# An attention and sign feed-forward kernel: three kinds of transposes leave TensorE, and the feed-forward is computed from three bf16 parts

## The chip, the cores and the metric

The kernel runs on one core of a Trainium2 chip. The time is that of one execution on the device, in microseconds (us). The names of the engines are those of the profile: PE is TensorE (PEld its weight loads), DVE is VectorE, ACT is ScalarE, POOL is GpSimd, SP is SyncE, which here only issues DMAs. Before the change the median of 3 runs is 4421.93 us (4421.24 to 4422.01).

## The reference

The input `x` has 4 batches of 2048 rows of 512 values, all in float32. There are 16 heads of 32 columns.

```python
q = (x @ Wq.T).reshape(N, S, H, hd).transpose(0, 2, 1, 3)      # k and v alike
attn = softmax(q @ k.T / sqrt(hd), axis=3)
x = layernorm(x + (attn @ v).transpose(0, 2, 1, 3).reshape(N, S, D))
w = (weights >= 0.0) * 2.0 - 1.0                               # 512 x 512, only +1 and -1
y = clip(einsum('bsi,oi->bso', x, w) * scale + bias, -100, 100)
out = layernorm(x + y)
```

`scale` and `bias` have one value for each of the 512 output columns.

## The kernel before

**Tiles and steps.** The work is cut into 16 groups `n` (4 batches of 4 groups of 4 heads), each group into 4 blocks `qb` of 512 queries, each block into 16 chunks `kc` of 128 keys. One chunk of one block is a *step*; there are 1024 steps, 64 to a group. The loop at the end of the function (L742 to L777) writes the instructions of one step after the other, and every engine works through its own in that order.

**What a step holds.** `scores` (L302) puts four banks of scores, transposed, into PSUM: a bf16 matmul that adds minus the row maximum, `negm`, and an f32 matmul of keys and queries. ACT turns them into `p` with four exponentials. `max_unit` (L236) computes scores once more, for a step 22 steps ahead (`LEAD`), the other way round, so that DVE can reduce each row to its maximum: three of the four banks are reduced out of PSUM, the fourth is first copied to SBUF (`moved`) by ACT. In every second step `weighted` (L323) multiplies two `p` by the values, and DVE adds the result to `oT`. POOL adds the `p` of a block up (`add_up`, L345), 14 additions of 128x2048 values for each 16 steps; of the sum and the last `p`, a matmul with ones makes the denominators.

PSUM has eight banks. `take` hands out the bank that a small model expects to be free first.

**Three things that are transposed on PE.** `max_rows` (L285) turns the maxima of a block, split by `max_parts` into three bf16 parts that are summed by the matmul, into `negm`: four bf16 transposes and an ACT copy. It stands three steps ahead of the block. `reciprocals` (L394) turns the denominators `dT` with four f32 transposes, so that DVE can take their reciprocals by query; `add_attention` (L410) turns `oT` likewise, multiplies, adds the columns of `x` and stores the result in DRAM (`res`). `Finish.turn` (L495) turns 128 rows for the feed-forward with four f32 transposes.

**The end of a batch.** `finish` (L550) spreads the rest of a batch, both layer norms and the feed-forward, over the steps of the next batch: 4 row tiles of 128 for each block, one tile each 13 steps (11 for the third batch). For a tile, `norm` (ACT), `turn` (PE, ACT), then three times `ffn` (L505), each a third of the output columns: four f32 matmuls, each of which the profile shows as two, and three DVE operations, of which each reads or writes the bank in PSUM. The signs of the weights are multiplied by `scale` beforehand by POOL (`sign_weights`, L145). The last batch has its own, denser plans: `finish_last` (L571) and, for its last block, `finish_end` (L600).

**Order.** `task` puts work on a list, with a first and a last step; `plan` (L680) deals it out to the steps: up to two *big* tasks (projections, thirds) and one *small* one in odd steps, a *col* task (denominators) in even ones. A third is kept apart from other thirds by `on_vector`. `at` fixes work to the end of a step. SP has the DMAs in program order; one that waits holds those behind it.

Of the kernel before, what the change touches and what calls it, by code (L numbers as in the profile page):

```python
# [20 lines left out]
def kernel(  # L21
# [13 lines left out]
    P = 128  # L35
# [21 lines left out]
    stage = ctx.enter_context(tc.tile_pool(name="stage", bufs=4))  # L57
# [9 lines left out]
    work = ctx.enter_context(tc.tile_pool(name="work", bufs=2))  # L67
# [37 lines left out]
    ident_bf = const.tile([P, P], BF16, name="ident_bf")  # L105
    nc.vector.tensor_copy(ident_bf, ident)
# [38 lines left out]
    def sign_weights():  # L145

        ws = raws["ws"]
        nc.gpsimd.tensor_scalar(ws, ws, 0.0, 2.0, ALU.is_ge, ALU.mult)
        for oc in range(DC):
            nc.gpsimd.tensor_scalar(  # L150
                ws[:, oc, :], ws[:, oc, :], 1.0, scale_t[:, oc : oc + 1], ALU.subtract, ALU.mult
            )

    raws = {n: load_weight(w, n) for n, w in (("wk", wk), ("wq", wq))}
    scale_t = const.tile([P, DC], F32, name="scale_t")
    bias_bc = const.tile([P, D], F32, name="bias_bc")

    def load_rest():
        for n, w in (("wv", wv), ("ws", w_ffn)):
            raws[n] = load_weight(w, n)  # L160
        nc.sync.dma_start(out=scale_t, in_=ffn_scale.rearrange("(c p) -> p c", p=P))
        nc.sync.dma_start(out=bias_bc, in_=ffn_bias.partition_broadcast(P))
# [15 lines left out]
    rec = {}  # L178

# [95 lines left out]
    def max_parts(n, qb, i):  # L275
        part = parts.pop((n, qb))
        nm = cols_of(i, NTQ, HG)
        sp = split[qb % 2]
        nc.vector.tensor_reduce(nm, part, AX.X, ALU.min)
        nc.vector.tensor_copy(sp[:, :, :, 0], nm)  # L280
        nc.vector.tensor_tensor(nm, nm, sp[:, :, :, 0], ALU.subtract)
        nc.vector.tensor_copy(sp[:, :, :, 1], nm)
        nc.vector.tensor_tensor(sp[:, :, :, 2], nm, sp[:, :, :, 1], ALU.subtract)

    def max_rows(n, qb):  # L285
        sp = split[qb % 2]
        i = take()
        pt = ps[:, i, : QB // 2].bitcast(BF16)
        for qc in range(NTQ):
            nc.tensor.transpose(  # L290
                pt[:, ts(qc, P)], sp[:, qc, :, :].rearrange("p h d -> p (h d)"), ident_bf
            )
        negm[n, qb] = small.tile([P, QB], BF16, tag="negm", name="negm")
        runs("full", 0.23)
        nc.scalar.copy(negm[n, qb], pt)
        give(i, "ACT", 0.6)
# [76 lines left out]
    def denominators(n, qb):  # L373

        if is_last(n, qb):
            b = sums[0]
        else:
            b = take()
            ones_times(b, last_p.pop((n, qb)), True, False)
            ones_times(b, acc.pop((n, qb)), False, True)  # L380
        dT = once.tile([P, QB], F32, tag="dT", name="dT")
        nc.scalar.copy(dT, ps[:, b, :])
        give(b, "ACT", 0.6)
        acc[n, qb] = dT

# [7 lines left out]

    def reciprocals(n, qb):  # L394
        i, pd = turn_back(acc.pop((n, qb)))
        rec[n, qb] = small.tile([P, NTQ, HG, 1], F32, tag="rec", name="rec")
        nc.vector.reciprocal(rec[n, qb], pd[:, :, :, 0:1])
        give(i, "DVE", 0.3)
# [30 lines left out]
    class Finish:  # L429
        def __init__(self, b, g):  # L430
            self.b, self.g = b, g
            self.mv, self.rs, self.nb, self.nT, self.rows_rs = {}, {}, {}, {}, {}

# [60 lines left out]

        def turn(self, j):  # L495
            i = take()
            pt = cols_of(i, DC, P)
            for c in range(DC):
                nc.tensor.transpose(pt[:, c, :], self.row(j)[:, ts(c, P)], ident)  # L499
            runs("full", 0.44)  # L500
            self.nT[j] = work.tile([P, DC, P], F32, tag="nT", name="nT", bufs=4)
            nc.scalar.copy(self.nT[j], pt)  # L502
            give(i, "ACT", 0.6)

        def ffn(self, j, third):  # L505
            cols = slice(0, D) if third is None else slice(THIRDS[third], THIRDS[third + 1])
            i = take()
            py = ps[:, i, : cols.stop - cols.start]
            for c in range(DC):
                nc.tensor.matmul(  # L510
                    py, lhsT=self.nT[j][:, c, :], rhs=wT["ws"][:, c, cols],
                    start=(c == 0), stop=(c == DC - 1),
                )
            runs("full", 6.8e-3 * (cols.stop - cols.start))
            nc.vector.tensor_tensor(py, py, bias_bc[:, cols], ALU.add)
            nc.vector.tensor_scalar(py, py, MAX_VAL, -MAX_VAL, ALU.min, ALU.max)
            dst = self.row(j)[:, cols]
            nc.vector.tensor_tensor(dst, dst, py, ALU.add)
            give(i, "DVE", 0.5 + 3.1e-3 * (cols.stop - cols.start))
# [30 lines left out]
    def finish(b, qb, a, every, w, lag):  # L550
        f = Finish(b, qb)
        at(a, f.load)
        for j in range(NTQ):
            at(a + 2 + j, f.stats, 1, j)
        at(a + 6, f.rstd, 1)
        at(a + 7 + lag, f.shift, 1)
        for j in range(NTQ):
            t = a + 8 + lag + every * j
            at(t, f.norm, 1, j)
            turned = task("small", t + 1, t + 3, f.turn, j)  # L560
            for k in range(3):
                task("big", t + 2, t + w, f.ffn, j, k, after=turned)
            at(t + w, f.stats, 2, j)
        e = a + 9 + lag + every * (NTQ - 1) + w
        at(e, f.rstd, 2)
        at(e + 1 + lag, f.shift, 2)
        for j in range(NTQ):
            at(e + 2 + lag + j, f.norm, 2, j)
        at(e + 5 + lag, f.store)

    def finish_last(qb, last):  # L571

        f = Finish(B - 1, qb)
        at(last - 9, f.load_last)
        a = last + 7
        late = qb == NQB - 2
        for j in range(NTQ):
            at(a + j // 2, f.stats, 1, j)
        at(a + 2, f.rstd, 1)
        at(a + 4, f.shift, 1)  # L580
        ffns = []
        for j in range(NTQ):
            t = a + 5 + (j if late else 2 * j)
            by = t + 6
            at(t, f.norm, 1, j)
            if late:
                by = total + (-1, 1, 4, 5)[j]
            turned = task("small", t + 1, t + 3, f.turn, j, after=ffns[j - 2] if j > 1 else None)
            for k in [None] if late else range(3):
                ffn = task("big", by if late else t + 2, by, f.ffn, j, k, after=turned)  # L590
            ffns.append(ffn)
            at(by + late, f.stats, 2, j)
        e = total + 7 if late else a + 18
        at(e, f.rstd, 2)
        at(e + 2, f.shift, 2)
        for j in range(NTQ):
            at(e + 3 + j, f.norm, 2, j)
        at(e + 7, f.store)

    def finish_end(qb, last):  # L600
# [10 lines left out]
        for j in range(NTQ):  # L611
            t = total + (6, 6, 7, 8)[j]
            turned = task("small", t, t, f.turn, j)
            t = total + 7 + j
            task("big", t, t, f.ffn, j, None, after=turned)
            at(t, f.stats, 2, j)
            at(t, f.rstd, 2, j, j + 1)
            at(t + 1, f.shift, 2, j, j + 1)
            at(t + 1, f.norm, 2, j)
            at(t + 1, f.store_tile, j)  # L620
# [7 lines left out]
    at(-8, sign_weights)  # L628
    for n in range(N):
# [28 lines left out]
        for qb in range(NQB):  # L658
# [3 lines left out]
            task("small", first - 3, first - 3, max_rows, n, qb)  # L662
# [4 lines left out]
            t = task("small", d + 1, d + 1 + w, reciprocals, n, qb, after=t)  # L667
            e = d + 2 if is_last(n, qb) else d + 3
            task("small", d + 2, e + w, add_attention, n, qb, after=t)
            if g == NG - 1:  # L670
                if b < B - 1:
                    every = 13 if b < B - 2 else 11
                    finish(b, qb, (b + 1) * NG * STEPS + qb * (5 * every - 1), every, every, 3)
                else:
                    (finish_end if is_last(n, qb) else finish_last)(qb, last)

    def on_vector(t):
        return t[3].__name__ == "ffn"

    def plan(quota=None):  # L680
# [9 lines left out]
        while any(len(gone[kind]) < len(tasks[kind]) for kind in tasks):  # L690
# [10 lines left out]
            for kind in most:  # L701
# [8 lines left out]
                if kind == "big" and middle:  # L710
                    if quota is not None and not heavy:
                        k = max(1, min(k, -(-quota[group] * (at_n + 1) // STEPS) - used[group]))


                    thirds = [t for t in can if on_vector(t)]
                    can = [t for t in can if not on_vector(t)]
                    if thirds and not can:
                        can = thirds[:1]
                    elif thirds and k == 2 and not heavy and not any(map(on_vector, must)):
                        can = thirds[:1] + can  # L720
                picked = must + can[: max(0, k - len(must))]
                for t in sorted(picked, key=lambda t: not on_vector(t)):
# [9 lines left out]
    for _ in range(4):  # L732
# [8 lines left out]
    s = start  # L741
    while s <= max(*chosen, *behind):  # L742
        now = None
# [70 lines left out]
```

## Time and profile before

| what | value |
|---|---|
| median of 3 runs | 4421.93 us |
| the profiled execution's own time | 4420.69 us |
| its span, first to last instruction | 4418.7 us |
| PE busy | 4380.8 us, 99% |
| POOL busy | 4083.3 us, 92%; 889 additions of 4.54 us are 4034.0 |
| DVE busy | 3320.2 us, 75% |
| ACT busy | 3048.4 us, 69% |
| granted PE clock | 0.999 |
| feed-forward matmuls on PE (L510) | 259.3 us busy |
| transposes on PE: rows (L499), sums and outputs (L390), maxima (L290) | 41.8, 83.6, 25.3 us busy |

Matmuls are pipelined, so that busy times of PE overlap and are longer than what a matmul adds to the chain. A group of instructions is told by its line, its engine and its tiles (`out<-in`). An idle time is put down to what ended it. The chain of work that ended last is followed back from the last instruction and shows what the time consists of.

### The profile page before, as it was taken

How to read it: one execution, taken by the hardware profiler on the slowest of the kernel's cores; microseconds unless marked ns; L12 is line 12 of the kernel's file. 1: busy time of each engine (PE TensorE's matmuls, PEld its weight loads, DVE VectorE, ACT ScalarE, POOL GpSimd, SP SyncE). 2: the span in 40 equal slices, each digit the busy share in tenths (PEclk: the TensorE clock that was granted, in tenths of full speed). 3: DMA queues.
4: the chain of work that ended last, by engine and by line, in shares of the span. 5: the costliest groups of instructions: out<-in, count | busy, mean ns of one | idle time of the engine just before them, and what ended most of it. 6: DMA issues, size and time to landing. Idle time of an engine off the chain costs nothing.

```text
span 4418.7 us, 94451 instructions
## 1 busy us (share of the span) xinstructions
PE 4380.8 (99%) x38648; PEld 2261.4 (51%) x38648; DVE 3320.2 (75%) x5909; ACT 3048.4 (69%) x6493; POOL 4083.3 (92%) x940
## 2 busy tenths in 40 slices
PE   9999999999999999999999999999999999999998
PEld 5554444454555555555555555555555555555443
DVE  6777777777777777777777777777777777777774
ACT  5666666676667667677676766767667676767675
POOL 3999999999999999999999999999999999999994
PEclk9999999999999999999999999999999999999999
DMA  3000000010000000011000000001000000000001
GB/s 91 6 11 11 6 11 11 9 39 28 6 11 30 6 20 20 6 42 32 20 20 6 30 11 16 20 7 48 16 20 20 18 18 20 16 20 30 13 23 45
DMA packets 98019, 92.30 MB, mean 21 GB/s; under 512 B 4272, under 2 KB 73904, under 8 KB 97584
## 3 DMA queue, kind: packets, MB, share of 16 engines
q1 hardware_dynamic: 92304, 82.07, 6.2%
q8 instruction: 302, 4.95, 0.5%
q10 hardware_dynamic: 5280, 4.19, 0.3%
q14 instruction: 133, 1.09, 0.1%
HBM read 53.74 MB, written 32.51 MB: 20 GB/s over the span
## 4 chain that ended last, share of the span: by engine, by line
PE 89%; POOL 8%; ACT 1%; issue 1%; DVE 1%; DMA 0%; ACTq 0%; POOLq 0%; DVEq 0%
PE ps L330 19%; PE ps L247 18%; PE ps L312 18%; PE ps L206 15%; POOL acc L350 8%; PE ps L306 7%; PE ps L510 5%; PE ps L356 3%; PE ps L390 2%; PE ps L499 1%; PE ps L195 1%; ACT p L319 1%; DVE part L254 1%; PE ps L290 0%; ACT xg_last L489 0%
## 5 line engine op out<-in xcount | busy, mean ns | idle before, releaser
L350 POOL TENSOR_TENSOR acc<-acc,p 128x2048 f32<-128x2048 f32 x825 | 3743.2, 4537 | 106.1 <-ACT p L319 49.3
L319 ACT ACTIVATE p<-ps 128x512 f32<-128x512 f32 x4096 | 2115.0, 604 | 1148.4 <-PE ps L312 1113.8
L254 DVE TENSOR_REDUCE part<-ps 128x1 f32<-128x512 f32 x3072 | 1934.8, 684 | 821.1 <-PE ps L247 820.2
L247 PE MATMUL ps<-kT,qT 32*128 32x512 f32 x8192 | 1098.1, 590 | 0.0
L312 PE MATMUL ps<-qT,kT 32*128 32x512 f32 x8192 | 1070.7, 590 | 0.0
L330 PE MATMUL ps<-p,vv 128*32 128x512 f32 x8192 | 983.6, 598 | 0.5 <-ACT p L319 0.3
L247 PEld LDWEIGHTS ps<-kT,qT 32*128 32x128 f32 x8192 | 524.0, 185 | 379.8 <-issue 221.0
L254 DVE TENSOR_REDUCE part<-moved 128x1 f32<-128x512 f32 x1024 | 691.2, 675 | 1.7 <-ACT moved L266 1.6
L266 ACT COPY moved<-ps 128x512 f32<-128x512 f32 x1024 | 634.5, 620 | 21.8 <-PE ps L247 16.7
L330 PEld LDWEIGHTS ps<-p,vv 128*32 128x32 f32 x8192 | 220.3, 109 | 685.6 <-issue 346.5
L306 PE MATMUL ps<-negm,ones_bf 32*128 32x512 bf16 x4096 | 434.9, 384 | 3.9 <-ACT p L319 1.3
L312 PEld LDWEIGHTS ps<-qT,kT 32*128 32x128 f32 x8192 | 405.6, 184 | 38.3 <-issue 20.4
L350 POOL TENSOR_TENSOR acc<-p 128x2048 f32<-128x2048 f32 x64 | 290.8, 4544 | 132.4 <-ACT p L319 132.3
L342 DVE TENSOR_TENSOR oT<-ps,oT 128x512 f32<-128x512 f32 x448 | 309.8, 692 | 90.1 <-PE ps L330 57.6
L306 PEld LDWEIGHTS <-ones_bf 32*128 32x128 bf16 x4096 | 104.3, 91 | 496.9 <-issue 438.3
L206 PEld LDWEIGHTS ps<-wvT,xT 128*128 128x128 f32 x2048 | 244.6, 191 | 67.7 <-ACT p L319 62.1
L206 PE MATMUL ps<-wvT,xT 128*128 128x128 f32 x2048 | 270.3, 280 | 1.4 <-ACT p L319 0.5
L206 PEld LDWEIGHTS ps<-xT,wkT 128*128 128x128 f32 x2048 | 242.4, 191 | 48.2 <-ACT p L319 46.7
L206 PE MATMUL ps<-xT,wkT 128*128 128x128 f32 x2048 | 265.1, 279 | 0.5 <-ACT p L319 0.2
L206 PE MATMUL ps<-xT,wqT 128*128 128x128 f32 x2048 | 262.2, 277 | 1.1 <-ACT p L319 1.0
L510 PE MATMUL ps<-wsT,nT 128*128 128x172 f32 (+2 forms) x1408 | 259.3, 329 | 2.4 <-ACT nT L502 1.1
L206 PEld LDWEIGHTS ps<-xT,wqT 128*128 128x128 f32 x2048 | 245.2, 192 | 25.5 <-ACT p L319 23.0
(74 smaller groups left out, 1831.2 us busy)
## 6 DMA issues: line engine op xcount, KB each, us to landing
xs<-in_L_attn_x_dram SPq DMA_DIRECT2D x64, 256.0 KB, 2.8
xc<-in_L_attn_x_dram SPq DMA_DIRECT2D x60, 256.0 KB, 3.2
res<-xc SPq DMA_DIRECT2D x60, 256.0 KB, 2.4
xg<-res SPq DMA_DIRECT2D x12, 1024.0 KB, 6.1
out_dram<-xg SPq DMA_DIRECT2D x12, 1024.0 KB, 4.8
xg_last<-res SPq DMA_DIRECT2D x4, 768.0 KB, 6.1
out_dram<-xg_last SPq DMA_DIRECT2D x3, 1024.0 KB, 4.3
raw_wk<-in_L_attn_Wk_dram ACTq DMA_DIRECT2D x4, 256.0 KB, 6.3
```

The lines of the kernel that those rows point to most:

```text
L206: nc.tensor.matmul(pp, lhsT=lhs(c), rhs=rhs(c), start=(c == 0), stop=(c == DC - 1))
L247: nc.tensor.matmul(ps[:, banks[h], :], lhsT=qT[n, qb][rows, ts(qc, P)], rhs=kT[n][rows, ts(kb, QB)], start=True, stop=True,)
L254: nc.vector.tensor_reduce(part[:, qc, h : h + 1, kb], src, AX.X, ALU.max, negate=True)
L266: nc.scalar.copy(moved, ps[:, banks[-1], :])
L306: nc.tensor.matmul(ps[:, banks[h], :], lhsT=ones_bf[rows, :], rhs=negm[n, qb][rows, :], start=True, stop=False,)
L312: nc.tensor.matmul(ps[:, banks[h], :], lhsT=kT[n][rows, ts(kc, P)], rhs=qT[n, qb][rows, :], start=False, stop=True,)
L319: nc.scalar.activation(p[:, h, :], ps[:, banks[h], :], AF.Exp, scale=SM_SCALE)
L330: nc.tensor.matmul(pb[cols, :], lhsT=vv[n][:, kc, cols], rhs=p[:, h, :], start=(i == 0), stop=(i == 1),)
L342: nc.vector.tensor_tensor(outs[n, qb], pb, outs[n, qb], ALU.add)
L350: nc.gpsimd.tensor_tensor(a, before if kc == 1 else a, p, ALU.add)
L356: nc.tensor.matmul(ps[h * HD : (h + 1) * HD, b, :], lhsT=ones, rhs=p[:, h, :], start=start, stop=stop,)
L510: nc.tensor.matmul(py, lhsT=self.nT[j][:, c, :], rhs=wT["ws"][:, c, cols], start=(c == 0), stop=(c == DC - 1),)
```

## The change

- **Maxima.** `max_parts` ends with a DMA transpose on SP's queue, 128x512 bf16, that writes `negm`. `max_rows`, its PE transposes and its ACT copy are gone.
- **Sums of the keys.** The denominators are copied over the first quarter of the sum's own tile; a DMA writes one row of each head to DRAM, a second reads them back as single values, turned. `reciprocals` stands two steps after the denominators. The last block of all keeps the PE transposes.
- **Feed-forward.** 56 of 64 row tiles: the normalized row is split into three bf16 parts (two ACT copies, two DVE subtractions), a DMA transposes all three (128x1536), and a third is 12 bf16 matmuls with the signs, which bf16 holds exactly. ACT copies a third to SBUF; three entries in the plan then scale it, add the bias and clip it, and add it to the row, on DVE. The last eight tiles keep the f32 way (`turn`, `ffn_whole`) with signs and scale in one.
- **Signs.** 12 DVE operations from step 80 on, in place of five of POOL's at the start.
- **Plan.** A tile each 12 steps (10 for the third batch), the pieces of a tile in steps of their own; the planner no longer treats thirds apart. `stage` has three buffers instead of four, `work` one instead of two.

```diff
-    stage = ctx.enter_context(tc.tile_pool(name="stage", bufs=4))
+    stage = ctx.enter_context(tc.tile_pool(name="stage", bufs=3))
-    work = ctx.enter_context(tc.tile_pool(name="work", bufs=2))
+    work = ctx.enter_context(tc.tile_pool(name="work", bufs=1))
...
+    def sign_weights(ic, k):
+        w = wT["ws"][:, ic, :]
+        if k == 0:
+            nc.vector.tensor_scalar(w, w, 0.0, 2.0, ALU.is_ge, ALU.mult)
+        elif k == 1:
+            nc.vector.tensor_scalar(ws_bf[:, ic, :], w, 1.0, None, ALU.subtract)
+        else:
+            nc.vector.tensor_tensor(w, ws_bf[:, ic, :], scale_bc, ALU.mult)
...
         nc.vector.tensor_tensor(sp[:, :, :, 2], nm, sp[:, :, :, 1], ALU.subtract)
-    def max_rows(n, qb):
...
+        nc.sync.dma_start_transpose(
+            out=negm[n, qb].rearrange("p (t q) -> p t q", t=NTQ),
+            in_=sp.rearrange("p t h d -> p (t h d)"),
+        )
...
+            dT = whole[:, 0, :]
         nc.scalar.copy(dT, ps[:, b, :])
         give(b, "ACT", 0.6)
         acc[n, qb] = dT
+        if not is_last(n, qb):
+            columns_of_sums(n, qb)
+            at(step[0] + 2, reciprocals, n, qb)
...
+    def columns_of_sums(n, qb):
+        dT = acc.pop((n, qb))
+        rows = dram.tile([HG, QB], F32, tag="sums", name="sums", bufs=2)
+        nc.sync.dma_start(out=rows, in_=dT.rearrange("(h r) q -> h r q", h=HG)[:, 0, :])
+        sums_of[n, qb] = small.tile([P, HG * NTQ], F32, tag="sums", name="sums")
+        with nc.allow_non_contiguous_dma(reason="2048 single sums"):
+            nc.sync.dma_start(
+                out=sums_of[n, qb], in_=rows.rearrange("h (t p) -> p (h t)", p=P)
+            )
...
+            by_head = sums_of.pop((n, qb)).rearrange("p (h t) -> p t h", h=HG)
+            nc.vector.reciprocal(rec[n, qb][:, :, :, 0], by_head)
...
+        def part_high(self, j):
+            self.parts[j] = work.tile([P, 3, D], BF16, tag="parts", name="parts")
+            nc.scalar.copy(self.parts[j][:, 0, :], self.row(j))
...
+        def less_high(self, j):
+            self.left[j] = work.tile([P, D], F32, tag="left", name="left")
+            nc.vector.tensor_tensor(
+                self.left[j], self.row(j), self.parts[j][:, 0, :], ALU.subtract
+            )
...
+        def part_middle(self, j):
+            nc.scalar.copy(self.parts[j][:, 1, :], self.left[j])
...
+        def part_low(self, j):
+            parts = self.parts.pop(j)
+            nc.vector.tensor_tensor(
+                parts[:, 2, :], self.left.pop(j), parts[:, 1, :], ALU.subtract
+            )
...
+            nc.sync.dma_start_transpose(
+                out=self.nT[j], in_=parts.rearrange("p k d -> p (k d)")
+            )
...
         def ffn(self, j, third):
+            cols = slice(THIRDS[third], THIRDS[third + 1])
+            i, py = self.times_weights(j, ws_bf, cols, 0.86)
...
+            nc.scalar.copy(self.y[j][:, cols], py)
+            give(i, "ACT", 0.3)
+
+        def scaled(self, j):
+            nc.vector.tensor_tensor(self.y[j], self.y[j], scale_bc, ALU.mult)
+
+        def clipped(self, j):
+            nc.vector.tensor_tensor(self.y[j], self.y[j], bias_bc, ALU.add)
+            nc.vector.tensor_scalar(self.y[j], self.y[j], MAX_VAL, -MAX_VAL, ALU.min, ALU.max)
+
+        def added(self, j):
+            nc.vector.tensor_tensor(self.row(j), self.row(j), self.y.pop(j), ALU.add)
...
+    def parted(f, t, j):
+        at(t, f.norm, 1, j)
+        at(t + 2, f.part_high, j)
+        at(t + 3, f.less_high, j)
+        at(t + 4, f.part_middle, j)
+        at(t + 5, f.part_low, j)
...
+            t = a + 13 + every * j
+            parted(f, t, j)
+            by = t + every - 1
             for k in range(3):
-                task("big", t + 2, t + w, f.ffn, j, k, after=turned)
+                task("big", t + 7, by, f.ffn, j, k)
+            at(by, f.scaled, j)
+            at(by + 2, f.clipped, j)
+            at(by + 3, f.added, j)
+            at(by + 4, f.stats, 2, j)
...
-            task("small", first - 3, first - 3, max_rows, n, qb)
...
-    def on_vector(t):
-        return t[3].__name__ == "ffn"
```

`times_weights` runs over the blocks of the transposed row, 12 of them for the three parts, and uses the same four blocks of weights for each part. In `finish_last` the first two blocks of the last batch do the same within fewer steps, a tile each three steps.

## The prediction

> **What bounds the kernel now.** The page comes first: engine totals and the chain that ended last, by engine.
>
> ```profile
> PE 4380.8 (99%) x38648; PEld 2261.4 (51%) x38648; DVE 3320.2 (75%) x5909; ACT 3048.4 (69%) x6493; POOL 4083.3 (92%) x940
> ...
> PE 89%; POOL 8%; ACT 1%; issue 1%; DVE 1%; DMA 0%; ACTq 0%; POOLq 0%; DVEq 0%
> ```
>
> PE carries the chain, but POOL has 8% of it, so some stage has another bound. To find it I cut the span at the first POOL addition of each group of heads (64 steps) and asked for the busy times of those stretches: columns PE, PEld, DVE, ACT, POOL.
>
> ```profile
> 611.80:869.80 258.00, 255.14 (x2292) 125.73 (x2288) 191.01 (x320) 176.79 (x376) 253.93 (x58) 1.00 0.03 9
> 1397.20:1666.50 269.30, 268.93 (x2402) 139.62 (x2401) 207.68 (x373) 187.74 (x401) 256.03 (x58) 1.00 0.06 17
> 1936.10:2211.90 275.80, 275.64 (x2467) 145.05 (x2466) 208.09 (x373) 195.56 (x417) 256.05 (x59) 1.00 0.11 32
> 3567.00:3839.90 272.90, 272.67 (x2420) 141.69 (x2418) 209.56 (x379) 188.97 (x403) 256.04 (x59) 1.00 0.06 19
> ```
>
> Groups 1 to 3 have no feed-forward and take 258 us: 56 additions of 4.54 us with 0.07 between them, POOL's own floor. Groups 4 to 14 carry the feed-forward of the batch before and take 267.5 to 276.3; PE is full there. POOL's floor for them is 258 plus two small `pow`, about 260. So at most some 10 us a group can be won.
>
> The rest is read from one step: the chain in order of time (start, us, what), then the timeline (start, us, engine, line).
>
> ```profile
> 1731.63 1.36 PE ps L510 x8
> ...
> 1742.13 1.17 PE ps L510 x8
> ...
> 1750.13 0.59 PE ps L390 x4
> ```
>
> ```profile
> 1746.26 1.89 DVE L254 TENSOR_REDUCE part<-ps 128x1 f32<-128x512 f32 x3 [1.06 <-PE ps L247]
> ...
> 1747.67 9.16 POOL L350 TENSOR_TENSOR acc<-acc,p 128x2048 f32<-128x2048 f32 x2 [0.21 <-ACT p L319]
> ...
> 1748.22 0.69 DVE L342 TENSOR_TENSOR oT<-ps,oT 128x512 f32<-128x512 f32 x1
> 1748.83 0.68 DVE L254 TENSOR_REDUCE part<-moved 128x1 f32<-128x512 f32 x1
> 1749.10 1.03 PE L247 MATMUL ps<-kT,qT 32*128 32x512 f32 x8
> ```
>
> Two things are to be seen. VectorE empties three of the four banks of maxima by 1748.15, and PE takes its next four at 1749.10: 0.95 us of room. What stands at the end of a step (`behind`) runs on VectorE after the last of these rows, at 1749.51, while the first of the two additions has 2.70 us to go. The same subtraction over 703 steps of groups 4 to 14 gives 2.17 us.
>
> A last pair of rows, from the timeline of the first microseconds:
>
> ```profile
> 1.24 0.98 POOL L119 MEMSET split<- 128x512 bf16 x2
> 1.32 0.98 DVE L106 CAST ident_bf<-ident 128x128 bf16<-128x128 f32 x1 [1.32 <-POOL ident masks.py:199]
> ```
>
> A cast of 128 columns, SBUF to SBUF, takes 0.98 us and ends at 2.30, just after POOL's memsets end at 2.22; VectorE's cast of 16 columns out of PSUM takes 0.23. The cast was held until POOL was done.
>
> **The change, part by part.** The profiled execution took 4420.69 us (span 4418.7, 2.0 around it), 1.2 below the median of 4421.93; the sum is made against 4420.69.
>
> *PE, removed.* In the chain a set of four maxima transposes (L290) has 0.33 us, of f32 transposes (L390, L499) 0.59. Each query block loses one L290 and one of its two L390: 0.92 us, 3.7 a group. 56 row tiles (48 of batches 0 to 2, 8 of batch 3) lose L499: 0.59. Eight others keep the f32 way.
>
> *PE, thirds.* Today 8 passes, 1.17 us (1.36 with a change of shape). New: 12 bf16 matmuls of 172 columns. L290's bf16 matmuls of 128 columns, each with its own weight load, follow each other every 0.056 us, so 172 columns take 0.075 and a third 0.90. From below 0.86 (no fixed part at all), from above 12 x 0.11 = 1.32 (the spacing of 128-column f32 transposes). I take 0.90, the same kind of instruction: 0.27 a third, 0.81 a tile.
>
> *Sum of the relief.* A group with four tiles: 3.7 + 4 x 1.4 = 9.3, so 269.3 becomes 260, POOL's floor. Group 4: 7.5; groups 5, 6, 8, 9, 10: 46.5; 7 and 11 (PE-bound at 275.8): 18.6; 12 to 14, five tiles each: 32; the last: 12; group 0: 3.7; groups 1 to 3 nothing, POOL bounds them. **120 us** in all.
>
> *VectorE's new work.* A tile today costs nine operations of 0.33 us, 3.0 us, every one with one operand in PSUM. New are five whole-row `tensor_tensor` (`less_high`, `part_low`, `scaled`, the bias, `added`), 0.69 each by L342, and a clip of 0.70 by its 128x512 form. All read and write SBUF alone, five of them from two SBUF tensors. No VectorE operation of the kernel before has that, so what it costs beside POOL is bounded by two rows. From below: nothing, as for L254 on `moved` (one SBUF input, 0.68, as fast as from PSUM). From above: L106, held until POOL's instruction ends. POOL adds 95% of the time in these stages, so this decides the case. I take the hold: L106 is the only row in which VectorE moves SBUF to SBUF elementwise while POOL runs.
>
> Price of one: wait 2.17, itself 0.69. Against it stand VectorE's idle time before the maxima, 821.1 us over 1024 steps, 0.80 a step, plus 0.25 (the 3.0 that go, over 12 steps), and the 0.95 of bank room. What PE loses: 2.86 - 1.05 - 0.95 = 0.86. Behind the waiting operation stand the next step's maxima, and PE waits for their banks. Four stand alone in their steps: 3.4. The bias and clip are a pair; if the clip follows at once, 0.86 + 0.70 = 1.56. **5.0 us a tile.** If POOL's next addition gets in between the pair, 4.54 more: 9.5. If PE had unlimited room, POOL would still stand still for 5 x 0.69 + 0.70 = 4.15 a tile, at a stage where it is at its floor: that is the lower end with a hold.
>
> The Trainium skill, "SBUF — State Buffer", section "Who interferes with whom", says that a VectorE instruction with two SBUF inputs contends with a GpSimd instruction that reads SBUF, the later one blocking until the earlier is through. Our row shows such a block only for a cast beside a memset; that two inputs do it no row here shows. By the rule the cost is the 5.0 a tile, by the most favourable row 0: 4621 or 4301 us.
>
> *Transposes of the parts (56).* 384 KB each on SP's queue. Nearest rows: 256 KB in 2.0 to 3.2 us to landing, up to 6.3 for a broadcast; no transpose is shown, so 2.0 to 6.3. `part_low` is issued at the end of step t+5 and PE may start the thirds in t+7, behind that step's scores and maxima: some 4.7 us later, of which `part_low` itself needs 0.69 and its wait 2.17. Left are 1.9 us, so 0.1 to 4.4 late, partly inside the stall already counted, partly put off by the planner. I take **0.5 a tile**.
>
> *Transposes of the maxima (64).* Issued five steps (21 us) before use, 128 KB: hidden by those steps even at 6.3. ACT loses L295's 0.645.
>
> *Sums through DRAM (63).* ACT copies, a DMA writes four rows (2.0 to 2.5), a second reads 2048 single values. 512 single values (`scale_t`) landed in 2.5; four times that is 10, and 4 if only what exceeds 2.0 grows. `reciprocals` stands two steps later, 9 us after the copy. I take 2.4 + 4 = 6.4: hidden. At 12.4 VectorE waits 3.4, PE loses 1.4, 88 us in all. SP holds the second until the first has landed; behind it stand only loads and stores due steps later.
>
> *Signs of the weights.* 12 VectorE operations in group 1, where POOL is the bound: 5 us if they only hold POOL up, 16 with stalls; I take 12. POOL's 15 us at the start end long before its first addition.
>
> *No cost:* `stage` with three buffers (xs lands in 2.8 us, transpositions are steps apart); 246 more issues on SP at 0.45; ACT's two copies and three thirds, +1.6 us a tile less 0.64 a block, beside 1114 us that it waits for PE; tighter steps of `finish`.
>
> **Sum:** 4420.7 - 120 + 56 x 5.5 + 12 = 4621, or **4622** against the median.
>
> **Rivals.**
> - *No hold (faster):* POOL and VectorE do not meet. 4421 - 120 = 4301. For it: reductions and statistics of SBUF data run undisturbed (0.68). Against it: L106. It decides below 120/56 = 2.1 us a tile.
> - *Only the clip is held,* the one new operation of L106's kind, one SBUF source to SBUF: 56 x 1 us back, 4357.
> - *The DMAs are late, nothing is held:* 4301 + 56 x 2.5 for the parts + up to 88 for the sums = 4440 to 4530.
> - *The bf16 thirds bring nothing:* at 1.32 a third the relief falls from 120 to about 50. L290's 0.056 speaks against.
> - *The pair is split by an addition:* 56 x 4.54 = 254 more, 4876.
>
> **How the numbers follow.** Hold in all six, 0.62: from 4533 (4421 - 120 + 56 x 4.15: POOL held, PE not) to 4876 (every pair split), likeliest 4622; of this 0.06 lies above 4830. DMAs late, 0.08. No hold, 0.20: 4290 to 4340. Clip alone, 0.10. A repeated measurement tells 0.2% from no change: 9 us. Faster 0.28, same 0.02, slower 0.70. The range goes from 4300 to 4830.
>
> **What would show it.** Right: in the windows of groups 4 to 14 the two-input VectorE rows average well over 1.5 us, PE waits for VectorE at L247 and L306, the groups take 280 to 295, POOL's share falls under 90%. Groups 2 and 3 stay at 258. A third shows 0.9 in the chain. Wrong: these rows at 0.69 and groups at 260 (no hold); PE waiting for a DMA into `nT`, or VectorE at `rec` (DMAs late). The weakest step is the room of 0.95 + 1.05.

## The result and the profile after

The changed kernel takes 4922.9 us (median of 4 runs, 4921.32 to 4935.17) beside 4421.59 before: a ratio of 1.114, 95% interval 1.1121 to 1.1159. The forecast of slower was right; 4622 and the range up to 4830 were too low. The profiled execution took 4935.17 us, with a span of 4933.4.

The page's engine totals, the granted clock in 40 slices of the span, and the chain by engine:

```profile
PE 4539.9 (92%) x38588; PEld 2279.2 (46%) x38588; DVE 4068.7 (82%) x5752; ACT 3097.8 (63%) x6653; POOL 4113.1 (83%) x935
...
PEclk9999999999999999999999999999999999999988
...
PE 60%; DVE 26%; issue 4%; POOL 4%; DMA 3%; ACT 2%; ACTq 0%; SPq 0%; DVEq 0%; POOLq 0%
```

PE is idle for 393.5 us (span less busy) in place of 37.9. VectorE is busy 748 us longer with fewer instructions, and now has a quarter of the chain, of which it had 1%. The digits of the clock hide what the list of clocks shows: a mean of 0.961 in place of 0.999.

The same cut as before, at the first POOL addition of a group (columns PE, PEld, DVE, ACT, POOL, then the clock):

```profile
349.80:626.00 276.20, 260.22 (x2271) 127.82 (x2273) 222.51 (x334) 175.36 (x375) 255.10 (x58) 0.99 0.06 11
626.00:884.00 258.00, 255.03 (x2272) 124.82 (x2264) 191.12 (x320) 174.85 (x372) 253.92 (x57) 1.00 0.06 12
...
1446.90:1751.50 304.60, 281.41 (x2400) 141.41 (x2399) 259.27 (x361) 194.40 (x421) 259.56 (x58) 0.96 0.10 22
...
4545.90:4933.40 387.50, 304.09 (x2218) 135.12 (x2216) 285.09 (x367) 210.38 (x456) 237.18 (x64) 0.88 0.15 37
```

Group 2, without feed-forward, still takes 258.0. Group 1, where the signs are made, takes 17.8 more than before. A group with feed-forward (group 5 is shown) takes 304.6 in place of 269.3, at a clock of 0.96. The last group, with eight new tiles in fewer steps, takes 387.5 in place of 306.0, at a clock of 0.88; that is 82 of the 515 us by which the span grew. So the loss lies where the new VectorE operations are, and nowhere else.

The groups of instructions (line, engine, operation, out<-in, count | busy us, mean ns) name them:

```profile
L532 DVE TENSOR_TENSOR parts<-left,parts 128x512 bf16<-128x512 f32 x56 | 204.8, 3657 | 2.6 <-ACT parts L527 2.5
L587 DVE TENSOR_SCALAR y<-y 128x512 f32<-128x512 f32 x48 | 175.8, 3662 | 1.6
L586 DVE TENSOR_TENSOR y<-y,bias_bc 128x512 f32<-128x512 f32 x48 | 159.0, 3312 | 0.0
L582 DVE TENSOR_TENSOR y<-y,scale_bc 128x512 f32<-128x512 f32 x48 | 148.3, 3090 | 0.0
...
L521 DVE TENSOR_TENSOR left<-xg,parts 128x512 f32<-128x512 f32 x48 | 92.1, 1919 | 0.0
...
L591 DVE TENSOR_TENSOR xg<-xg,y 128x512 f32<-128x512 f32 x48 | 67.8, 1413 | 0.0
```

One row of 512 values takes 0.69 us where nothing is in the way; here it takes 1.4 to 3.7. The clip's durations by themselves tell the rest (min/median/max ns):

```profile
L587 DVE TENSOR_SCALAR y<-y x48: 426/4618/4761, 1228.5 to 4579.6; 128x512 f32<-128x512 f32 x48
```

It takes 0.43 us, or one POOL addition longer. The timeline of one such place (start, us, engine, line; in brackets idle time and what ended it):

```profile
1632.73 14.10 POOL L344 TENSOR_TENSOR acc<-acc,p 128x2048 f32<-128x2048 f32 x3
...
1634.78 1.03 PE L306 MATMUL ps<-qT,kT 32*128 32x512 f32 x8
...
1635.06 2.74 DVE L586 TENSOR_TENSOR y<-y,bias_bc 128x512 f32<-128x512 f32 x1
...
1637.84 4.62 DVE L587 TENSOR_SCALAR y<-y 128x512 f32<-128x512 f32 x1
...
1642.38 1.87 DVE L255 TENSOR_REDUCE part<-ps 128x1 f32<-128x512 f32 x3
1643.11 0.61 PE L300 MATMUL ps<-negm,ones_bf 32*128 32x512 bf16 x2 [4.28 <-DVE part L255]
...
1643.12 2.31 PE L306 MATMUL ps<-qT,kT 32*128 32x512 f32 x8
```

Two of POOL's three additions end at 1637.26 and 1642.18; the bias ends 0.54 us after the first, the clip 0.28 after the second. Behind them stands the reduction that frees PE's banks; PE is idle for 4.28 us. And when it goes on, the eight matmuls that took 1.03 us at 1634.78 take 2.31. The granted clock of these microseconds (third column from the end) is 0.56:

```profile
1643.00:1646.50 3.50, 3.39 (x18) 1.94 (x17) 3.50 (x6) 1.22 (x3) 3.50 (x1) 0.56 0.00 0
```

### The profile page after: what moved, and what is told of

Its sections match the earlier page's. It is cut to its first block, busy times and chain, and to the rows that moved or that the text cites. A ratio compares the mean times of both kernels' runs of the same rounds, so it can differ in the third digit from the quotient of the medians.

```text
span 4933.4 us, 94802 instructions
## 1 busy us (share of the span) xinstructions
PE 4539.9 (92%) x38588; PEld 2279.2 (46%) x38588; DVE 4068.7 (82%) x5752; ACT 3097.8 (63%) x6653; POOL 4113.1 (83%) x935
## 4 chain that ended last, share of the span: by engine, by line
PE 60%; DVE 26%; issue 4%; POOL 4%; DMA 3%; ACT 2%; ACTq 0%; SPq 0%; DVEq 0%; POOLq 0%
PE ps L248 14%; PE ps L306 13%; PE ps L324 13%; DVE part L255 11%; PE ps L207 9%; PE ps L300 5%; POOL acc L344 4%; DVE parts L532 3%; PE ps L562 3%; DMA nT<-parts 3%; DVE y L586 3%; DVE y L582 2%; PE ps L350 2%; ACT p L313 1%; DVE y L587 1%
## 5 line engine op out<-in xcount | busy, mean ns | idle before, releaser
L344 POOL TENSOR_TENSOR acc<-acc,p 128x2048 f32<-128x2048 f32 x825 | 3787.4, 4591 | 337.6 <-ACT p L313 282.7
L255 DVE TENSOR_REDUCE part<-ps 128x1 f32<-128x512 f32 x3072 | 1931.8, 682 | 640.7 <-PE ps L248 639.1
L248 PE MATMUL ps<-kT,qT 32*128 32x512 f32 x8192 | 1238.5, 616 | 22.4 <-DVE part L255 11.8
L306 PE MATMUL ps<-qT,kT 32*128 32x512 f32 x8192 | 1150.0, 615 | 0.0
L248 PEld LDWEIGHTS ps<-kT,qT 32*128 32x128 f32 x8192 | 586.8, 191 | 451.3 <-issue 215.3
L300 PE MATMUL ps<-negm,ones_bf 32*128 32x512 bf16 x4096 | 506.5, 390 | 296.1 <-DVE part L255 262.7
L255 DVE TENSOR_REDUCE part<-moved 128x1 f32<-128x512 f32 x1024 | 690.9, 675 | 5.4 <-ACT moved L267 5.3
L300 PEld LDWEIGHTS <-ones_bf 32*128 32x128 bf16 x4096 | 117.1, 91 | 800.5 <-issue 740.1
L306 PEld LDWEIGHTS ps<-qT,kT 32*128 32x128 f32 x8192 | 422.1, 190 | 77.3 <-issue 60.5
L207 PE MATMUL ps<-wvT,xT 128*128 128x128 f32 x2048 | 282.4, 290 | 2.0 <-DVE part L255 2.0
L207 PE MATMUL ps<-xT,wkT 128*128 128x128 f32 x2048 | 276.8, 287 | 4.3 <-DVE part L255 4.0
L532 DVE TENSOR_TENSOR parts<-left,parts 128x512 bf16<-128x512 f32 x56 | 204.8, 3657 | 2.6 <-ACT parts L527 2.5
```

Of the source, the lines that this page charges most:

```text
L207: nc.tensor.matmul(pp, lhsT=lhs(c), rhs=rhs(c), start=(c == 0), stop=(c == DC - 1))
L248: nc.tensor.matmul(ps[:, banks[h], :], lhsT=qT[n, qb][rows, ts(qc, P)], rhs=kT[n][rows, ts(kb, QB)], start=True, stop=True,)
L255: nc.vector.tensor_reduce(part[:, qc, h : h + 1, kb], src, AX.X, ALU.max, negate=True)
L300: nc.tensor.matmul(ps[:, banks[h], :], lhsT=ones_bf[rows, :], rhs=negm[n, qb][rows, :], start=True, stop=False,)
L306: nc.tensor.matmul(ps[:, banks[h], :], lhsT=kT[n][rows, ts(kc, P)], rhs=qT[n, qb][rows, :], start=False, stop=True,)
L344: nc.gpsimd.tensor_tensor(a, before if kc == 1 else a, p, ALU.add)
```

## The experiments

Shares below are of the kernel before in the same comparison, where there were several rounds. All but the two delays and the control start from the changed kernel or from parts of it.

**Without POOL's additions.** In `add_up`, of both kernels:

```diff
-        if 0 < kc < (NT // 2 if is_last(n, qb) else NT - 1):
+        if kc == 1:
             a = acc[n, qb]
```

> The changed kernel with 13 of POOL's 14 additions of each block left out (the sums are those of the first two chunks and of the last, so the denominators are wrong). Theory of the hold (a VectorE operation that reads two SBUF tensors, or runs SBUF to SBUF with one, stands until POOL's addition is over): the six operations of a tile fall from 1.4 to 3.7 us each to 0.4 to 0.7, the granted clock goes back to 1.00, the groups with feed-forward fall from 305 us to 262 or less, the time to 4300 or less. If instead these operations are slow by themselves, or the late transposes of the parts are what stalls PE, they keep over 1.4 us or the groups stay over 285, and the time stays over 4600.

> The kernel before with the same additions left out, as a control for the run without them of the changed kernel. POOL's floor of 258 us a group goes with them, so groups 1 to 3 may fall to what PE needs, 245 to 256; groups 4 to 14 were bound by PE at 267 to 276 and should stay there. Hold theory: 4390 to 4420, so 90 to 130 above the changed kernel without additions. Were the additions themselves what slows PE here, groups 4 to 14 would fall too.

The changed kernel falls from 4922.9 to 4357.65 us, the control from 4421.1 to 4403.02. The clock is at 0.998. Of the changed kernel's rows without the additions:

```profile
L532 DVE TENSOR_TENSOR parts<-left,parts 128x512 bf16<-128x512 f32 x56 | 75.0, 1340 | 2.5 <-ACT parts L527 2.5
...
L591 DVE TENSOR_TENSOR xg<-xg,y 128x512 f32<-128x512 f32 x48 | 32.7, 680 | 0.0
...
L587 DVE TENSOR_SCALAR y<-y 128x512 f32<-128x512 f32 x48 | 20.5, 427 | 1.7
```

The clip and `added` have their plain durations. `part_low` (L532) and the bias (1.38 us) are above theirs: one addition in 14 is left, and they still meet it in some blocks. 565 us go with the other 13, and only 18 in the control, so the additions beside the new VectorE operations are the cause. But the time is 58 us over the expected 4300, group 5 takes 264.7 us in place of 262 or less, and the changed kernel is only 45 us below the control, where 90 to 130 were expected: the relief of PE is smaller than worked out. That is taken up below.

**POOL writes and does not read.** The additions become a short addition and a memset of the whole sum:

```diff
-            nc.gpsimd.tensor_tensor(a, before if kc == 1 else a, p, ALU.add)
+            nc.gpsimd.tensor_tensor(a[:, :, :4], p[:, :, :4], p[:, :, :4], ALU.add)
+            nc.gpsimd.memset(a, 1.0)
```

> The changed kernel with POOL's additions replaced by an addition of 4 columns of each head and a memset of the whole sum, which only writes (the sums of the keys are wrong then). If it is POOL's reading of SBUF that holds a VectorE operation with two SBUF inputs, the four plain ones (scaled, bias, left, added) fall to 0.7 us, while the clip, one input and SBUF to SBUF, stays held and over 1 us. If any POOL instruction holds all of them, all six stay over 1 us for as long as a memset lasts. If none is held, all are at 0.4 to 0.7.

```profile
L345 POOL MEMSET acc<- 128x2048 f32 x889 | 1604.7, 1805 | 52.9
...
L533 DVE TENSOR_TENSOR parts<-left,parts 128x512 bf16<-128x512 f32 x56 | 38.1, 681 | 2.5 <-ACT parts L528 2.5
...
L587 DVE TENSOR_TENSOR y<-y,bias_bc 128x512 f32<-128x512 f32 x48 | 32.7, 680 | 0.0
...
L588 DVE TENSOR_SCALAR y<-y 128x512 f32<-128x512 f32 x48 | 27.9, 581 | 1.7
```

4341.87 us. All operations with two SBUF inputs are at 0.66 to 0.68, also beside a memset. The clip is not over 1 us, against the expectation, since little of a memset was left where it began. Yet it is held: of its 56 executions all that began while a memset ran had 0.18 to 0.55 us of it before them, and took that rest and 0.28 us more (0.46 to 0.82); the others took 0.43. So there are two kinds. An operation with two SBUF inputs waits for a POOL instruction that reads SBUF. An elementwise one from SBUF to SBUF with a single input, as the clip is, and the cast L106 in the kernel before was, also waits for one that only writes. This is what the Trainium skill, "SBUF — State Buffer", section "Who interferes with whom", states of the two, and here both halves of it have their rows. Reductions and statistics of SBUF data, which have one input too, are not held: in the changed kernel, beside the additions, they take 0.68 us (L255 on `moved`, L481).

**Four of the six operations out of PSUM.** The thirds are scaled, biased, clipped and added from their bank, as before the change; the two subtractions of the split stay in SBUF:

```diff
-            nc.scalar.copy(self.y[j][:, cols], py)
-            give(i, "ACT", 0.3)
+            nc.vector.tensor_tensor(py, py, scale_bc[:, cols], ALU.mult)
+            nc.vector.tensor_tensor(py, py, bias_bc[:, cols], ALU.add)
+            nc.vector.tensor_scalar(py, py, MAX_VAL, -MAX_VAL, ALU.min, ALU.max)
+            dst = self.row(j)[:, cols]
+            nc.vector.tensor_tensor(dst, dst, py, ALU.add)
```

> The changed kernel with scale, bias, clip and addition done by thirds with one operand in PSUM, four VectorE operations of 0.33 us a third as before the change; only the two subtractions of the split still read two SBUF tensors. Hold theory: four of six held operations go, with about two thirds of the waiting; groups with feed-forward fall from 305 to 272 to 285, the time to 4480 to 4620. If the late transposes of the parts were the larger cause, the groups stay over 295 and the time over 4800.

4637.55 us, 1.0492 (1.0475 to 1.0510): 285 us less, a little above the expected range. The groups come to 277 to 296. The two subtractions took 2.95 and 3.21 us, so what was moved stopped waiting and what was not moved went on:

```profile
L532 DVE TENSOR_TENSOR parts<-left,parts 128x512 bf16<-128x512 f32 x56 | 179.7, 3209 | 0.8 <-ACT parts L527 0.7
L521 DVE TENSOR_TENSOR left<-xg,parts 128x512 f32<-128x512 f32 x48 | 141.7, 2952 | 0.0
...
L573 DVE TENSOR_TENSOR ps<-ps,scale_bc 128x172 f32<-128x172 f32 x112 | 38.0, 339 | 19.2 <-PE ps L562 19.1
```

**Two delays of VectorE in the kernel before,** to price a delay by itself. From step 128 on, in each 12 steps, two reductions of resident values, six steps apart or directly after one another:

```diff
+    def hold_vector():
+        nc.vector.tensor_reduce(
+            idle, wT["wk"].rearrange("p c o -> p (c o)"), AX.X, ALU.max
+        )
+    for k in range(128, total, 12):
+        for more in (0, 6):
+            at(k + more, hold_vector)
```

> The kernel before, unchanged in what it computes, with VectorE held up on purpose from step 128 on: in each 12 steps two reductions of 2048 resident values (about 2.3 us each by the 0.675 of 512), six steps apart. One SBUF input, so POOL is not met. By the room of before (0.80 + 0.95 = 1.75 us a step) PE loses about 0.5 us at each of 150: 4500, with the clock still at 1.00. If VectorE's lateness had no room at all, 4770; if the lateness of VectorE costs PE nothing, 4421.

> The same reductions, the two of each 12 steps directly after one another, so one delay of 4.6 us at 75 places. By the room alone PE stands still 2.85 us each time: 4421 + 214 = 4635, clock 1.00. If, as I now think, a standstill of PE of this length also brings a stretch of about 3.4 us at half the clock, another 1.7 us each time: 4760, granted clock 0.97 or less. That would be the part that the prediction left out.

Split: 4593.17 us, clock 0.999. The kernel before took 4422.35 beside it. The reductions take 2.28 us, and 171 us over 150 of them are 1.14 each, so the room is 1.14 us and not 1.75. Together: 4764.56 us, clock 0.974, with the same VectorE work. PE's idle time is 243 us, 205 more than before. The mean clock is 0.974 in place of 0.999, which over the span is some 120 us at most. These two make 325 of the 342 us. With the 120 taken out, a delay of 4.56 us costs 2.96 (222 over 75), so by this run the room is 1.6. One place, in windows of the columns used above and in the timeline:

```profile
1415.00:1420.00 5.00, 2.23 (x20) 1.56 (x12) 4.96 (x4) 2.19 (x5) 4.92 (x2) 0.92 0.00 0
1420.00:1426.00 6.00, 5.98 (x30) 3.16 (x31) 2.83 (x7) 1.83 (x5) 2.27 (x1) 0.50 0.01 3
1426.00:1432.00 6.00, 6.00 (x58) 3.41 (x55) 5.17 (x9) 3.69 (x9) 5.14 (x2) 0.99 0.00 0
```

```profile
1414.77 4.60 DVE L625 TENSOR_REDUCE idle<-wkT 128x1 f32<-128x2048 f32 x2
...
1420.02 2.08 PE L206 MATMUL ps<-xT,wqT 128*128 128x128 f32 x8 [2.79 <-DVE part L254]
1422.03 0.61 PE L306 MATMUL ps<-negm,ones_bf 32*128 32x512 bf16 x4
1422.43 1.92 PE L312 MATMUL ps<-qT,kT 32*128 32x512 f32 x8
```

PE stands 2.79 us, then runs 6 us at a clock of 0.50, during which it is busy without a break and does 30 matmuls in place of 58. POOL is not met here at all. A delay of 4.6 us thus costs 4.56, more than what is left of it after the room; two of half the length cost half as much together, with the clock untouched. Not every standstill brings the half clock: PE stands for over 2 us 73 times in this run, and 54 of these are followed by half the clock.

**Thirds two steps later.**

```diff
-                task("big", t + 7, by, f.ffn, j, k)
+                task("big", t + 9, by, f.ffn, j, k)
```

> The changed kernel with the thirds allowed two steps later (t + 9 in place of t + 7), everything else as it is. If the late transposes of the parts are a small part (0.5 us a tile, the term of the prediction), the time falls by 20 to 60, to about 4870; PE's waits for nT (67 us in the changed kernel) go. If they were the main part of the 11 us a tile, it falls by over 200, below 4720.

4907.92 us, 15 less, just under what was expected of a small part. PE's waits, in the changed kernel

```profile
PE ps L300 <- DVE part L255: 262.7, 125, 6.0
...
PEld L562 <- DMA nT<-parts: 50.4, 40, 2.6
...
PE ps L562 <- DMA nT<-parts: 16.2, 38, 1.8
```

(us in total, times, longest), lose those for `nT`, and those for VectorE stay: 273 in place of 263 us at L300. The transposes were late, and it hardly mattered.

**The clip in a step of its own.**

```diff
             at(by + 2, f.clipped, j)
-            at(by + 3, f.added, j)
-            at(by + 4, f.stats, 2, j)
+            at(by + 3, f.cut, j)
+            at(by + 4, f.added, j)
+            at(by + 5, f.stats, 2, j)
```

> The changed kernel with the clip in a step of its own, one step behind the bias, and the addition one step later; everything else as it is. In the changed kernel the clip takes 3.66 us because POOL's next addition gets in between the bias and the clip, and both delays fall into one step. Apart, VectorE's two delays have two steps' room: 2 to 4 us less a tile, 4740 to 4830. If the number of held operations alone counts, not how they lie, the time stays within 30 us of 4923.

`cut` is the clip alone; `clipped` keeps the bias. 4843.64 us, 79 less, and 14 us above the range. The clip's mean falls from 3.66 to 1.71 us, while the two operations next to it rise (`added` from 1.41 to 2.19, `less_high` from 1.92 to 3.21). How the held operations lie counts, but spreading them does not end the holds.

**Only the two turns.** The kernel before, with `max_rows` and the denominators' transposes replaced as in the change and nothing else.

> The kernel before with only the DMA transpose of the maxima and the way of the sums through DRAM; feed-forward, plan and buffers are those of before. It adds no VectorE operation on two SBUF tensors. Theory: each block loses 0.92 us of PE, 3.7 a group, groups 4 to 14 go from 269.5 to 266, the time to about 4375 (0.990). If the round trip of the sums is late (VectorE waiting for it before the reciprocal), up to 88 us come back and the kernel is no faster, 4380 to 4460.

4375.18 us, 0.9896 (0.9882 to 0.9911), as worked out: 1.0% below the kernel before, and faster than both kernels. Groups 2 and 5, windows as above:

```profile
608.00:866.10 258.10, 254.00 (x2260) 124.49 (x2256) 191.16 (x320) 174.85 (x372) 254.02 (x58) 1.00 0.06 12
1389.60:1655.70 266.10, 266.10 (x2370) 137.81 (x2369) 207.37 (x373) 185.85 (x397) 256.05 (x58) 1.00 0.08 19
```

VectorE never waits for a DMA of the sums in this run, so their way through DRAM is hidden.

**All of the change without held operations.** The row goes into a bank of PSUM (ACT), both subtractions start from there, the thirds as two experiments earlier, the signs from POOL at the start and from ACT:

```diff
+            self.left[j] = take()
+            rest = ps[:, self.left[j], :]
+            nc.scalar.copy(rest, self.row(j))
+            nc.vector.tensor_tensor(rest, rest, self.parts[j][:, 0, :], ALU.subtract)
...
+            nc.scalar.copy(parts[:, 1, :], rest)
+            nc.vector.tensor_tensor(parts[:, 2, :], rest, parts[:, 1, :], ALU.subtract)
```

> All three parts of the change, with no VectorE operation on two SBUF tensors and none from SBUF to SBUF: the row is copied into a bank of PSUM by ACT, both subtractions of the split have their first operand there, scale, bias, clip and addition go by thirds out of PSUM, and the signs are made by POOL at the start and by ACT. Hold theory: clock 1.00, no VectorE operation over 0.8 us, groups 4 to 14 at 262 to 268, the time 4310 to 4385, so as good as the two turns alone (4375) or better. If the DMA of the parts is late enough to matter by itself, or the bank that is held costs PE, 4385 to 4480.

> The version with everything out of PSUM, with two things changed about its banks: the split of a row (copy, subtraction, cast, subtraction) is done at the end of one step, so its bank is not held into the next, and the planner keeps thirds apart again as before the change, so that two thirds do not wait for VectorE in one step. In the version before, the maxima's matmuls took 1.86 us in place of 0.86 in such steps, 30.7 us in two groups. If that was the banks, groups 4 to 14 go from 277 to 262 to 268 and the time to 4310 to 4390. If it is the additional VectorE and ACT work as such, it stays at 4450 to 4520.

The first takes 4511.62 us, 1.0201 (1.0184 to 1.0218), the second 4580.53, 1.0366 (1.0349 to 1.0384). Both miss. No row operation waits for POOL any more (0.68 us), and the first has the full clock. But PE waits for banks, as the chain of the first shows at the maxima (L252):

```profile
1708.76 0.33 PE ps L304 x4
1709.09 0.86 PE ps L310 x8
1709.94 1.86 PE ps L252 x7
```

Two of the pieces called thirds (24 matmuls) stand just before these rows. The likely reason is that a bank that VectorE keeps longer leaves the maxima a bank whose exponentials ACT has not yet done: PE's weight loads for the maxima wait 104 us for ACT's exponentials, in the kernel before 7.5.

```profile
PEld ps L252 <- ACT p L317: 104.2, 186, 2.6
```

My repair, the split within one step and thirds apart, made it worse: copy, subtraction, cast and subtraction wait for one another across two engines, PE waits 76 us for the last of them, its idle time rises from 58 to 129 us, and the mean clock falls from 0.998 to 0.988.

```profile
PE ps L252 <- DVE parts L538: 75.8, 52, 2.2
```

So this form of the feed-forward did not pay here without held operations either; whether another order would make it pay was not tried.

## Why the prediction was right and wrong

- *What bounds the kernel.* Right: groups 2 and 3 stay at POOL's floor (258.0, 258.8), and the two turns alone come out at 4375.18 for an expected 4375.
- *The hold.* Right: with 13 of 14 additions gone 565 us go. But the row L106 that decided for it could not show it for five of the six operations. It is a cast with one input beside a memset, and the memset run shows that operations with two inputs do not wait for a memset. From that row alone the right answer was luck.
- *The pair.* I let the clip follow the bias at once. It did not: its median is a whole addition, 4.62 us. This was named as a rival at 254 us; setting it apart was worth 79.
- *The room.* Taken as 2.0 us (1.75 in the kernel before), and named as the weakest step; the delays measure 1.1 and 1.6. It was the gap to the next taking of banks plus VectorE's mean idle time; that both are not always there together is likely, but not shown.
- *PE's standstill.* 5.0 and 0.5 us a tile were put down. Measured: 355.6 us more idle, 15.1 of them in group 1, so 340.5/56 = 6.1 a tile. That this is near is luck: the room was too large and the pair was split, and either makes the term larger. Nor is it all of the standstill: with the split delays, which cost 171 us, idle time grows by only 96 and PE's busy time by 77, at the full clock.
- *What failed: "What PE loses: 2.86 - 1.05 - 0.95".* The term that it leads to, 5.5 us a tile and 308 in all, was too small: with the relief and the signs as measured, the tiles cost 4922.9 - 4421.6 + 61 - 17.8 = 544.5 us, 9.7 a tile. The step priced a standstill at its own length; the half clock after it was in no term. Mean clock 0.961 over 4933.4 us is 192 us lost, 0.001 of 4418.7 is 4 before: 188 us, 3.4 a tile. This is the most it can be, since some 30 us of it fall on time in which PE stands anyway. Of the 69 stretches at half the clock 36, with about half of the loss, follow the held bias and clip. That the clock falls after a standstill is shown without POOL, by the joined delays.
- *The relief.* 120 us were put down. Without holds the change is 45 (one addition left) or 61 us (memset) below the control. In the memset run two groups lose 20.6 us of PE for thirds and transposes, 10.3 a group, as worked out (9.3), but other matmuls take 4.7 a group more. Part of it is read from the order of PE's records: the first 128-row matmul behind the maxima ends 0.31 us after them, a second one 0.11 after the first; with the transposes gone, projections open such a stretch 322 times in place of 175, some 29 us. My 0.59 for four transposes held such an opening, which passes to the next where other 128-row matmuls follow. This is read from records and not tested: with only the two turns replaced, 3.5 of the expected 3.7 us a group came. The last group, with eight tiles in fewer steps, is 8 us longer than the control's. What else is in it was not separated.
- *Sum by what was measured:* 4421 - 61 + 340 + 15 + 188 = 4903 of 4923. It closes better than its terms allow: the 30 us are counted twice, and what the idle time does not show of the standstills is left out. How the 9.7 a tile divide between standstill and half clock is known only roughly.
- *Small terms.* Signs: 12 expected, 17.8 in group 1. A third: 0.90 expected, 0.87 in the chain (`1616.97 0.87 PE ps L562 x12`). Groups 4 to 14: 280 to 295 expected as a sign of the hold, 301.5 to 330.9 measured. Late transposes of the parts: 28 expected, 15 by moving the thirds. Maxima and sums: hidden, as expected.

The rivals fall: holds are real, they hold all six, and the DMAs are late by little.

## What to carry to other kernels

Where POOL works without a pause, each VectorE operation that reads two SBUF tensors, or goes from SBUF to SBUF elementwise with one, has to be priced at what is left of POOL's instruction, and a second one behind it at a whole instruction; one operand in PSUM avoids that but costs bank time, which needs its own price. A delay has to be priced twice: what is over the room as time that PE stands, and, if PE stands some 2 us or more, mostly 3.4 or 6.8 us at half the clock after it; in one run shorter standstills brought it too. In the changed kernel each of the 43 standstills of over 3 us was followed by such a stretch. And a change of several parts is best priced part by part, since here two cheap turns were worth 1.0% and lay hidden under the third part's loss.

## What the runs showed of the hardware that was not expected

- The clock falls to 0.50 for stretches that the list of clocks gives as 3.4 or 6.8 us, four times 10.2: 69 of them in the changed kernel before its last microseconds, 54 with the joined delays, none with the split ones, where PE never stood for 2 us. But 2 us is no bound. The second version without held operations has 26 such stretches before its last microseconds, PE never stands there for over 2.23 us, and before most of them it stands for less than 2.
- A clip that begins beside a POOL memset ends 0.28 us after it, while a `tensor_tensor` of two SBUF inputs beside the same memsets takes its plain 0.68.
- A DMA transpose of 128x1536 bf16 (384 KB) takes 3.7 us from its issue to its landing, in the chain of the changed kernel at 1604.72.
